# One pool of four 2 KB rooms in place of a pool of three and a pool of one, in a transformer block with an attention and an NF4 feed-forward half

## The chip, the cores and the metric

The kernel runs on one core of one Trainium2 chip. The metric is the device time of one execution in microseconds (us). Of the kernel before there are three timed runs: 3039.47, 3035.39 and 3045.34 us, median 3039.47. One further execution was profiled; all rows below are from it.

## What is computed

One block over a sequence of S = 2048 rows of E = 1024 values, in float32. First half: layer norm, attention with 16 heads of 64 values (rotary positions on queries and keys, causal mask), output projection, layer norm, and the residual. Second half: layer norm, a gated feed-forward layer with I = 2752 whose weights are stored as 4-bit codes with a scale for each 64 of them, layer norm, residual.

```
q, k, v = x @ Wq, x @ Wk, x @ Wv          # 16 heads of 64
q, k    = x*cos + rotate_every_two(x)*sin
out     = softmax(causal(q @ k.T) / 8) @ v   -> @ Wo
W       = NF4[codes] * scales             # gate, up, down
y       = (silu(h @ Wg.T) * (h @ Wu.T)) @ Wd.T
x = x + layernorm(attention(layernorm(x)));  x = x + layernorm(ffn(layernorm(x)))
```

## The kernel before, in words

Every float32 product is done as two or three matmuls on a high and a low part: `split` (L117) makes the parts, the high one by a ScalarE copy and the low one by a VectorE subtraction; `mm3` (L110) issues the three matmuls.

**Rooms.** On-chip memory is divided by hand into tags (`SLOTS`, L70); each tag has a number of rooms of one size. `slot` (L74) asks for a room. Two tags have rooms of 2 KB a partition:

- `t2`, three rooms: `t1` and `sh`, the work of the rotary embedding in `qkv` (L229 to L246); the five lookup lines `ln` of each `looked_up` (L512 to L518); the scales of the first gate and up weights (L550); `u` of the last, half-filled tile (L582).
- `ol`, one room: `ol`, the sum of the two halves of a head's weighted values (L316 to L319), written by ScalarE, added to by VectorE and stored by a DMA; the codes of the first gate and up weights (L550); `s3`, a difference of two gated tiles, made by GpSimd and stored by a DMA (L597 to L599).

The banks of PSUM are tags too (L71): `F` has one bank, for the products of `qkv` and for their transposes; `O` has one, for the weighted values; `S` and `T` have three each.

**What sets the order.** The program is traced in the order of the text. When it is built, a scheduler plays it against a timeline and fixes a static order for each engine: an instruction goes as soon as its engine, its inputs and its rooms are there, the earlier one in the text first. The rooms of one tag are given out in the order in which the text first writes the tiles: a tile doesn't get a room before each earlier tile of its tag has had one, even while rooms stand empty. On the chip, each engine runs its own instructions in that static order.

**Attention.** Eight pairs of heads. For each head and each 512-column block J of queries, `attend` (L365) runs `scores` (L252: products, mask, maxima on VectorE, exponentials on ScalarE, normalisation on GpSimd) and then `weighted` (L303): transposes of the probabilities, `split` into `pw`, products into bank `O`, then `ol`. A pair has eight `ol` tiles.

Between these lie the q, k and v products of later pairs. A *group* is the three products of one pair m and one 512-row block c (`group`, L374; `qkv`, L219). Each product fills bank `F`, is copied to `t1`, and goes on through rotary work to a store; `load_x` fetches its input into the four `xc` rooms. In the pairs 0 to 5 the groups stand in the text after all eight attends of their pair (L407 to L413), and `pace` (L409) spreads their first matmuls over that pair's scores:

```
for i, (m, c) in enumerate(now):
    ...
    group(m, c, None if i or own else ready, pace)
```

So the text of a pair has eight `ol` tiles first, and then five `t1` and `sh` tiles for each of three groups (four in pair 0). Pairs 6 and 7 have single groups between their attends (L396, L437), pair 6 two more at its end. Pair m can start only when the groups of m have stored their keys: the groups (4,3), (5,3) and (6,0) are those of the pairs 3, 4 and 5.

**Output projection**, then x2, the transposed input of the second half (L424 to L561).

**Gate and up.** 22 tiles n. For each, `gate_up` (L565) runs for four blocks c: two products of 24 matmuls each, Silu, product, store. For n even it also makes `s3` after c = 1 and c = 3. The loop that sets the order of the text is

```
for n in range(NIT):
    if n < NIT - 2:
        for c in range(NC):
            gate_up(*todo[n], c)
    if n + 1 < NIT:
        now, steps = gate_up_weights(n + 1)
        todo.append(now)
        for step in steps:
            step()
    for j in range(2):
        down_weights(n // 2, 2 * (n % 2) + j)
```

Each step of `gate_up_weights` is one `looked_up` with five `ln` tiles and a `split`; a tile n has four of them, and two more in `down_weights`. **Down** (L739) are seven products of a Strassen-like scheme on the stored tiles; it uses neither tag.

Of the kernel before, what the change touches and what calls it, by code (L numbers as in the profile page):

```python
# [10 lines left out]
F32 = mybir.dt.float32  # L11
# [11 lines left out]
D = 64  # L23
I = 2752
P = 128
# [27 lines left out]
def it_cols(it):  # L53
    return 256 if it < NIT - 1 else 128
# [3 lines left out]
def block_kernel(ctx, tc, x, wq, wk, wv, wo, gu_codes, gu_scales, d_codes, d_scales, cos_sin, out):  # L58
# [8 lines left out]
    ps = ctx.enter_context(tc.tile_pool(name="ps", bufs=1, space=PSUM))  # L67


    SLOTS = {"hd": (7, 8), "w": (3, 8), "xc": (4, 8), "pa": (6, 8), "pb": (2, 4), "f4": (4, 4), "pw": (3, 4), "t2": (3, 2), "ol": (1, 2)}  # L70
    BANKS = {"F": 1, "S": 3, "T": 3, "O": 1}  # L71
    BANK_ORDER = ("F", "S", "S", "S", "T", "T", "T", "O")

    def slot(tag, shape, dtype, name):  # L74
        assert int(np.prod(shape[1:])) * 4 <= SLOTS[tag][1] * 1024, (tag, shape)
        return sb.tile(shape, dtype, tag=tag, name=name, bufs=SLOTS[tag][0])

    def bank(tag, name="bk"):
        return ps.tile([P, 512], F32, tag=tag, name=name, bufs=BANKS[tag])
# [3 lines left out]
    def any_bank():  # L83
        turn[0] += 1
        return bank(BANK_ORDER[turn[0] % 8])
# [24 lines left out]
    def mm3(o, w, xx, first, last):  # L110

        r = T.matmul(o, lhsT=w[:, 0], rhs=xx[:, 0], start=first, stop=False)  # L112
        T.matmul(o, lhsT=w[:, 0], rhs=xx[:, 1], start=False, stop=False)  # L113
        T.matmul(o, lhsT=w[:, 1], rhs=xx[:, 0], start=False, stop=last)  # L114
        return r

    def split(hi, lo, src):  # L117
        A.copy(hi, src)  # L118
        return V.tensor_tensor(lo, src, f32(hi), ALU.subtract)  # L119
# [183 lines left out]
    def weighted(h, J, prob, v):  # L303
        o = bank("O", "o")
        nk = 4 * J + 4
        for kb in range(nk):
            j0 = max(0, kb - 4 * J)
            pt = bank("T", "pt")
            for j in range(j0, 4):
                T.transpose(pt[:, j * P : (j + 1) * P], prob[kb // 4][:, j, kb % 4 * P : (kb % 4 + 1) * P], ident)  # L310
            cs = slice(j0 * P, 512)
            pw = slot("pw", [P, 2, 512], FR, "pw")
            split(pw[:, 0, cs], pw[:, 1, cs], pt[:, cs])
            T.matmul(o[:, cs], lhsT=v[:, kb, :], rhs=pw[:, 0, cs], start=kb == 0, stop=False)  # L314
            T.matmul(o[:, cs], lhsT=v[:, kb, :], rhs=pw[:, 1, cs], start=False, stop=kb == nk - 1)  # L315
        ol = slot("ol", [D, 512], F32, "ol")  # L316
        A.copy(ol, o[D:P, :])
        V.tensor_tensor(ol, o[:D, :], ol, ALU.add)
        load(at[J][h * D : (h + 1) * D, :], ol)  # L319
# [45 lines left out]
    def attend(h, J, q, k, v, anchors):  # L365
        weighted(h, J, scores(J, q, k, anchors), v)
# [12 lines left out]
    for pair in range(KE - 1):  # L379
        anchors = []  # L380
        now = [later[g] for g in range(len(later)) if g * (KE - 1) // len(later) == pair]
# [115 lines left out]
    def looked_up(codes, s0, s1, rows, tags=None, m=None):  # L497

        if tags:
            c8, sc = (slot(tag, [P, 512], F32, "cs") for tag in tags)  # L500
        else:
            cs = slot("pw", [P, 2, 512], F32, "cs")
            c8, sc = cs[:, 0], cs[:, 1]
        for r in range(0, P, rows):
            load(c8[r : r + rows].bitcast(I32), codes)
        load(sc[:D], s0.partition_broadcast(D))
        load(sc[D:], s1.partition_broadcast(D))
        if m is None:
            m = slot("f4", [P, 2, 512], F32, "m")[:, 0]
        V.tensor_scalar(c8, c8.bitcast(I32), 1.0, -8.0, ALU.mult, ALU.add)  # L510

        def line(ab):  # L512
            ln = slot("t2", [P, 512], F32, "ln")
            if ab[2] == 1.0:
                A.activation(ln, c8, AF.Identity, bias=bias_of[ab], scale=ab[0])
            else:
                A.activation(ln, c8, AF.Prelu, bias=bias_of[ab], scale=ab[0], alpha=ab[2])  # L517
            return ln  # L518

        low = line(CODES_6_8)  # L520
        V.scalar_tensor_tensor(m, line(CODES_9_12), CODES_9_12[3], low, ALU.add, ALU.max)
        V.scalar_tensor_tensor(m, line(CODES_2_5), CODES_2_5[3], m, ALU.add, ALU.min)
        V.tensor_tensor(m, m, line(CODES_0_1), ALU.min)
        V.scalar_tensor_tensor(m, line(CODES_13_15), CODES_13_15[3], m, ALU.add, ALU.max)  # L524
        V.tensor_tensor(m, m, sc, ALU.mult)
        return m

    def gate_up_weights(n, tags=None):
        it = PAIRS[n]
        w = it_cols(it)  # L530
        wt = [slot(tag, [P, 2, 4, w], FR, "wt") for tag in ("hd", "pa" if n % 2 else "hd")]
        kk = 512 // w

        def columns_of(k0):
            n = kk * w
            off = it * KE * 256 + k0 * w
            t = wt[k0 // 4][:, :, k0 % 4 : k0 % 4 + kk, :]
            m = looked_up(
                gu_codes[:, off : off + n], gu_scales[0:1, off : off + n], gu_scales[1:2, off : off + n], P, tags
            )  # L540
            split(t[:, 0].rearrange("p k n -> p (k n)"), t[:, 1].rearrange("p k n -> p (k n)"), m)

        return (it, wt, w), [partial(columns_of, k0) for k0 in range(0, KE, kk)]
# [3 lines left out]
    new_x2(0, ["hd"] * 4)  # L547
    new_x2(1, ["pa"] * 4)
    fills = list(range(8))
    now, steps = gate_up_weights(0, ("ol", "t2"))  # L550
    todo = [now]
    for t in range(NEWX, NT):
        project_out(t, False)
# [11 lines left out]
    def gate_up(it, wt, w, c):  # L565
        g = any_bank()

        def product(o, a):
            for k in range(KE):
                mm3(o, wt[k // 4][:, :, k % 4, a : a + P], x2[c][k], k == 0, k == KE - 1)  # L570

        product(g, 0)
        kt, later, grp, odd = it % half, it // half, c // 2, c % 2
        if (kt, later, grp) not in rooms:
            rooms[kt, later, grp] = slot("f4" if later else "pb", [P, 2, 512], F32, "in")
        inter = rooms[kt, later, grp][:, odd]
        rows = P if w == 256 else D
        if w == 256:
            u = any_bank()
            product(u, P)  # L580
        else:
            u = slot("t2", [P, 512], F32, "u")[:D]  # L582
            A.copy(u, g[D:P])
            G.memset(inter[D:], 0.0)
        A.activation(inter[:rows], g[:rows], AF.Silu)  # L585
        V.tensor_tensor(inter[:rows], u, inter[:rows], ALU.mult)
        have.add((kt, grp, later, odd))

        def keep(name, tile_):
            load(aq[name][kt][:, grp], tile_)  # L590

        if (later, odd) != (0, 1):
            keep(("A11", "A12", "A22")[later + odd], inter)

        first = rooms[kt, 0, grp]
        if later == 0 and {(kt, grp, 0, 1 - odd)} <= have:
            s3 = slot("ol", [P, 512], F32, "s3")  # L597
            G.tensor_tensor(s3, first[:, 0], first[:, 1], ALU.subtract)
            keep("S3", s3)  # L599
        if {(kt, grp, a, b) for a in range(2) for b in range(2)} <= have:  # L600
            second = rooms[kt, 1, grp]
            G.tensor_tensor(first[:, 1], first[:, 1], second[:, 1], ALU.add)
            keep("S1", first[:, 1])
            G.tensor_tensor(first[:, 0], first[:, 1], first[:, 0], ALU.subtract)
            keep("S2", first[:, 0])
            G.tensor_tensor(second[:, 0], second[:, 0], first[:, 0], ALU.subtract)
            keep("S4", second[:, 0])
# [35 lines left out]
# [11 lines that stand above are left out]
# [20 lines left out]
    for c in (1, 0, 2, 3):  # L674
        for it in todo[NIT - 2 :]:
            gate_up(*it, c)
        if c == 0:

            for kt in range(2):
                ready["A11", kt] = fetch("A11", "B11", kt, True)  # L680
# [123 lines left out]
```

## Time and profile before

| What | Value |
|---|---|
| Median of the three runs | 3039.47 us |
| The profiled execution | 3038.32 us |
| Its span, first to last instruction | 3036.5 us |
| Granted TensorE clock, mean | 0.988 |
| Busy: PE, VectorE (DVE), ScalarE (ACT), GpSimd (POOL) | 96%, 67%, 56%, 31% |
| Start of the first attend's `ol`, end of the last | 188.5, 1511.6 us |
| `s3`, first and last | 1680.2, 2599.4 us |
| PE busy in 1680 to 2500 us (gate and up) | 820.0 of 820.0 us |

The span is 1.8 us shorter than the execution's own time. In the rows, PE is TensorE's matmuls, PEld its weight loads; Lnnn is the line of the kernel; "SPq" is the queue from which nearly all DMAs are issued. In a list of what waited, "x <- y: us, times" is the idle time of x's engine that y ended.

### The profile page before, as it was taken

The numbers are of one execution on the slowest core, as the hardware profiler recorded it, in microseconds if no ns is written. First come the engines' busy times: TensorE is split into PE (matmuls) and PEld (weight loads), VectorE is DVE, ScalarE is ACT, GpSimd is POOL, SyncE is SP. The second block draws the span as 40 slices with busy tenths as digits, with TensorE's granted clock in tenths as the row PEclk, the third lists the DMA queues.
The fourth block names the chain that finished last, engine by engine and source line by source line (L and its number), as shares of the span: only waits on it lengthen the run. The fifth ranks groups of instructions, "written<-read, shape, count | busy, mean of one in ns | idle before, by whom it ended". The sixth has DMA issues, their size and how long they took to land.

```text
span 3036.5 us, 42534 instructions
## 1 busy us (share of the span) xinstructions
PE 2918.4 (96%) x14168; PEld 2409.9 (79%) x14168; DVE 2033.8 (67%) x4171; ACT 1699.7 (56%) x3569; POOL 955.5 (31%) x1055
## 2 busy tenths in 40 slices
PE   7989999999999999989989999999999999899998
PEld 6868888787877787778767888888888888788887
DVE  6567778777867777777565666776666668344347
ACT  4256667676766666676555555665555556232234
POOL 5344344443444443453322122222221213100034
PEclk9999999999999999999999999999999999999999
DMA  8787666656557557472356344444433445644446
GB/s 292 270 264 233 205 212 196 192 191 205 155 193 200 191 169 229 137 241 81 104 191 215 122 139 135 152 137 134 143 122 130 137 138 180 215 136 152 146 146 232
DMA packets 271740, 536.01 MB, mean 177 GB/s; under 512 B 22944, under 2 KB 113056, under 8 KB 255648
## 3 DMA queue, kind: packets, MB, share of 16 engines
q1 hardware_dynamic: 269344, 529.10, 54.1%
q10 hardware_dynamic: 2176, 4.19, 0.4%
q8 instruction: 112, 1.84, 0.3%
q14 instruction: 108, 0.88, 0.1%
HBM read 371.98 MB, written 161.22 MB: 176 GB/s over the span
## 4 chain that ended last, share of the span: by engine, by line
PE 78%; DMA 9%; DVE 6%; ACT 3%; issue 2%; POOL 1%; SPq 0%; POOLq 0%; ACTq 0%; DVEq 0%
PE bk L112 13%; PE bk L114 13%; PE bk L113 13%; PE pt L310 6%; PE qkv L112 5%; PE qkv L113 5%; PE qkv L114 5%; PE o L315 4%; PE o L314 3%; PE s L268 3%; PE s L270 3%; DMA wf<-in_wq 2%; DMA xc<-xd 1%; PE pj L458 1%; PE pj L456 1%
## 5 line engine op out<-in xcount | busy, mean ns | idle before, releaser
L300 POOL TENSOR_SCALAR prob<-prob,rc 128x512 f32<-128x512 f32 (+3 forms) x640 | 406.0, 657 | 434.1 <-DVE rc L295 231.1
L113 PE MATMUL bk<-x,wt 128*128 128x512 f32 x1376 | 535.6, 389 | 0.0
L114 PE MATMUL bk<-x,wt 128*128 128x512 f32 x1376 | 535.2, 389 | 0.0
L112 PE MATMUL bk<-x,wt 128*128 128x512 f32 x1376 | 533.6, 389 | 1.1 <-ACT wt L118 0.9
L278 ACT ACTIVATE prob<-s,mxs 128x512 f32<-128x512 f32 (+3 forms) x640 | 402.5, 632 | 146.1 <-DVE mxs L276 91.5
L119 DVE TENSOR_TENSOR pw<-pt,pw 128x512 fp32r<-128x512 f32 (+3 forms) x640 | 378.3, 601 | 121.8 <-ACT pw L118 120.1
L118 ACT CAST pw<-pt 128x512 fp32r<-128x512 f32 (+3 forms) x640 | 324.1, 527 | 171.6 <-PE pt L310 141.0
L517 ACT ACTIVATE ln<-cs,bias 128x512 f32<-128x512 f32 x520 | 359.6, 716 | 108.0 <-DVE m L524 23.4
L310 PE MATMUL pt<-ident,prob 128*128 128x128 f32 x2176 | 346.1, 275 | 6.2 <-DVE pw L119 4.9
L310 PEld LDWEIGHTS pt<-ident,prob 128*128 128x128 f32 x2176 | 267.9, 142 | 61.2 <-issue 6.6
L112 PEld LDWEIGHTS bk<-x,wt 128*128 128x128 f32 x1376 | 258.2, 188 | 55.4 <-ACT wt L118 1.9
L114 PEld LDWEIGHTS bk<-x,wt 128*128 128x128 f32 x1376 | 258.3, 188 | 53.8
L113 PEld LDWEIGHTS bk<-x,wt 128*128 128x128 f32 x1376 | 258.2, 188 | 53.5
L276 DVE TENSOR_REDUCE mxs<-s 128x1 f32<-128x512 f32 x384 | 260.8, 681 | 59.4 <-PE s L270 58.0
L268 PE MATMUL s<-k,q 128*128 128x512 f32 (+3 forms) x640 | 265.0, 415 | 22.8 <-ACT prob L278 20.1
L315 PE MATMUL o<-pw,v 128*128 128x512 f32 (+3 forms) x640 | 247.3, 388 | 11.2 <-DVE pw L119 10.6
L314 PE MATMUL o<-pw,v 128*128 128x512 f32 (+3 forms) x640 | 244.2, 382 | 9.2 <-ACT pw L118 7.2
L112 PE MATMUL bk<-bt,at 128*128 128x512 f32 x616 | 239.9, 391 | 9.9 <-ACT in L585 8.2
L112 PE MATMUL qkv<-xc,w 128*128 128x512 f32 x576 | 230.9, 401 | 11.9 <-ACT w L179 6.8
L113 PE MATMUL bk<-bt,at 128*128 128x512 f32 x616 | 240.6, 391 | 0.0
L114 PE MATMUL bk<-bt,at 128*128 128x512 f32 x616 | 239.7, 391 | 0.0
L270 PE MATMUL s<-k,q 128*128 128x512 f32 (+3 forms) x640 | 235.6, 370 | 0.0
(146 smaller groups left out, 5512.8 us busy)
## 6 DMA issues: line engine op xcount, KB each, us to landing
xc<-xd SPq DMA_DIRECT2D x96, 1024.0 KB, 9.1
q<-qs SPq DMA_DIRECT2D x128, 256.0 KB, 7.0
ast<-S SPq DMA_DIRECT2D x44, 512.0 KB, 3.9
cs<-in_gu_scales SPq DMA_DIRECT2D x172, 128.0 KB, 3.2
cs<-in_gu_codes SPq DMA_DIRECT2D x86, 256.0 KB, 3.0
A<-in SPq DMA_DIRECT2D x66, 256.0 KB, 2.0
S<-in SPq DMA_DIRECT2D x66, 256.0 KB, 3.2
ast<-A SPq DMA_DIRECT2D x33, 512.0 KB, 4.5
```

What stands on the lines that cost most here:

```text
L112: r = T.matmul(o, lhsT=w[:, 0], rhs=xx[:, 0], start=first, stop=False)
L113: T.matmul(o, lhsT=w[:, 0], rhs=xx[:, 1], start=False, stop=False)
L114: T.matmul(o, lhsT=w[:, 1], rhs=xx[:, 0], start=False, stop=last)
L119: return V.tensor_tensor(lo, src, f32(hi), ALU.subtract)
L268: mm = T.matmul(s, lhsT=q[:, 0, j * P : (j + 1) * P], rhs=k[:, b:e], start=True, stop=False)
L270: T.matmul(s, lhsT=q[:, 1, j * P : (j + 1) * P], rhs=k[:, b:e], start=False, stop=True)
L278: A.activation(prob[i][:, j, : e - b], s, AF.Exp, bias=mx, scale=sign, accum_out=sums[:, j % BATCH, i : i + 1])
L300: G.tensor_scalar(p, p, rc[:, jj % BATCH, i : i + 1], 0.0, ALU.mult, ALU.add)
L310: T.transpose(pt[:, j * P : (j + 1) * P], prob[kb // 4][:, j, kb % 4 * P : (kb % 4 + 1) * P], ident)
L314: T.matmul(o[:, cs], lhsT=v[:, kb, :], rhs=pw[:, 0, cs], start=kb == 0, stop=False)
L315: T.matmul(o[:, cs], lhsT=v[:, kb, :], rhs=pw[:, 1, cs], start=False, stop=kb == nk - 1)
L517: A.activation(ln, c8, AF.Prelu, bias=bias_of[ab], scale=ab[0], alpha=ab[2])
```

## The change

`ol` is dropped as a tag. Its one room goes to `t2`, which has four, and its three users ask for `t2`. Nothing else is changed: the same instructions on the same engines, the same memory.

```
-    SLOTS = {"hd": (7, 8), "w": (3, 8), "xc": (4, 8), "pa": (6, 8), "pb": (2, 4), "f4": (4, 4), "pw": (3, 4), "t2": (3, 2), "ol": (1, 2)}
+    SLOTS = {"hd": (7, 8), "w": (3, 8), "xc": (4, 8), "pa": (6, 8), "pb": (2, 4), "f4": (4, 4), "pw": (3, 4), "t2": (4, 2)}
...
-        ol = slot("ol", [D, 512], F32, "ol")
+        ol = slot("t2", [D, 512], F32, "ol")
...
-    now, steps = gate_up_weights(0, ("ol", "t2"))
+    now, steps = gate_up_weights(0, ("t2", "t2"))
...
-            s3 = slot("ol", [P, 512], F32, "s3")
+            s3 = slot("t2", [P, 512], F32, "s3")
```

## The prediction

> **What bounds the kernel now.** I read the page, then the chain that ended last, then what waits around `ol`, then windows of the stages. The page gives PE as the bound: busy for 96% of the span, 78% of the chain.
>
> ```profile
> PE 2918.4 (96%) x14168; PEld 2409.9 (79%) x14168; DVE 2033.8 (67%) x4171; ACT 1699.7 (56%) x3569; POOL 955.5 (31%) x1055
> ...
> PE 78%; DMA 9%; DVE 6%; ACT 3%; issue 2%; POOL 1%; SPq 0%; POOLq 0%; ACTq 0%; DVEq 0%
> ```
>
> So all idle time of PE is 3036.5 - 2918.4 = 118 us. What the one `ol` room costs is in the list of what waited around that tile:
>
> ```profile
> L317 ACT COPY ol<-o x64: 582/584/589, 188.5 to 1511.6; 64x512 f32<-64x512 f32 x64
> ...
>   DMA at<-ol: 11.8, 5
> ...
> DMA to landing us min/median/max: 2.2/6.2/12.4
> ```
>
> Five of 64 copies wait for the last store, 11.8 us of ScalarE. PE's gaps just behind these and two shorter waits (0.59, 2.00, 2.24, 0.99, 0.74, 0.58, 0.53 us) are 7.7 us. That is all there is to win there.
>
> Next, three stretches that a pair of heads each takes (columns: start and end, length, then busy PE, PEld, DVE, ACT, POOL with counts, granted clock, DMA share, GB/s):
>
> ```profile
> 541.00:695.00 154.00, 151.50 (x831) 127.82 (x831) 118.34 (x304) 104.37 (x278) 67.93 (x92) 0.98 0.63 192
> 695.00:855.00 160.00, 153.24 (x821) 125.86 (x822) 121.57 (x316) 109.14 (x290) 66.27 (x93) 0.98 0.62 188
> 855.00:1021.00 166.00, 154.61 (x825) 125.78 (x826) 121.36 (x317) 109.43 (x293) 66.70 (x94) 0.99 0.61 184
> ```
>
> Of the mean 153 us of PE, the nine q, k, v products (24 matmuls each, 0.23 us from start to start) are 50 us and their transposes 1.5; attention is about 101. These 50 us are what PE does while it waits for VectorE and ScalarE.
>
> **The rule that decides.** Rooms of a tag go out in the order of the text. The queue shows it, around the first lookups:
>
> ```profile
> 1335.50 1.04 SPq L507 DMA_DIRECT2D cs<-in_gu_scales  x1
> ...
> 1512.97 0.45 SPq L319 DMA_DIRECT2D at<-ol  x1
> 1515.24 0.34 SPq L505 DMA_DIRECT2D cs<-in_gu_codes  x1
> ...
> 1524.45 0.49 SPq L506 DMA_DIRECT2D cs<-in_gu_scales  x1
> ```
>
> The scales of step 1 take a `t2` room at 1335, when the last `t1` has had its own. Those of step 2 need nothing, and two of three rooms stand empty for 180 us, yet they come only at 1524, when the lines of step 1 (the first at 1518.4) have had their rooms. So in the pool of four every `t1`, `sh` and `ln` queues behind each earlier `ol` and `s3`, whatever is free. The number of rooms hardly matters; the order does.
>
> **Part 1, `s3` among the lookup lines.** In the text, `s3` of the last block of an even tile n stands before the lines of n+1. Now they run the other way round (n = 2):
>
> ```profile
> 1752.85 1.32 ACT L517 ACTIVATE ln<-cs,bias 128x512 f32<-128x512 f32 x2
> ...
> 1784.03 0.71 ACT L517 ACTIVATE ln<-cs,bias 128x512 f32<-128x512 f32 x1
> ```
> ```profile
> 1794.13 1.29 POOL L598 TENSOR_TENSOR s<-in 128x512 f32<-128x512 f32 x1 [2.83 <-issue]
> ```
>
> All six steps (30 lines in 31 us, 5.1 us a step) end 10 us before that `s3`. With one pool they come behind it, that is, behind the last product of tile n, while PE wants the weights of n+1 at once. PE's wait for the first step: the product L586 0.68, five VectorE operations L521 to L525 at 0.68, ScalarE's copy L118 0.60, some seven hand-overs of 0.1: 5.4 us, and up to 1 us for lines in between: 6.5. Below: 5.4, if ScalarE has all lines ready. Above: 9, if no line starts before `s3` itself. The later steps come at 5.1 us each, while one step's weights give PE 8 products x 6 matmuls x 0.23 = 11 us in eight banks: no further wait. PE has nothing else to do in this stage; VectorE and ScalarE, 69% and 56% busy in 1680 to 2500, have room for the shifted work, and what stands behind the lines on ScalarE (Silu of later blocks) isn't held up, since the order is made so that the lines are placed later rather than waited for. The loads of codes and scales are in other rooms (`pw`) and stay early on the queue; the store of `s3` stays where it is. It happens for n = 0, 2 to 18: ten times; for odd n there is no `s3`.
>
> After such a gap the matmuls are slow. The nearest row:
>
> ```profile
> 2601.07 0.39 PE L113 MATMUL bk<-bt,at 128*128 128x512 f32 x1
> 2609.68 0.80 PE L112 MATMUL bk<-bt,at 128*128 128x512 f32 x1 [8.22 <-ACT in L585]
> ...
> 2614.54 0.63 PE L113 MATMUL bk<-bt,at 128*128 128x512 f32 x1
> ...
> 2615.26 0.39 PE L112 MATMUL bk<-bt,at 128*128 128x512 f32 x1
> ```
>
> 5.6 us at a granted clock of 0.50: 13 matmuls in the time of 24, a loss of 2.6 us. The Trainium skill ("TensorE: Matmul & The Clock Gate", section "What's actually happening") has full clock again after some 3.4 us of work, a loss of 1.7. By the rule ten stalls would cost 17 us more, by the row 26; I take the row. Sum: 10 x (6.5 + 2.6) = 91 us (54 + 17 = 71 to 90 + 26 + ten slips of 2 = 136).
>
> **Part 2, `ol` among the rotary rooms.** A pair's eight `ol` stand before its groups' `t1`. So the first product of a pair fills the one bank `F` and waits there for the last attend; the other eight come in a bunch behind it. Now the products of such a pair are spread evenly (the `t1` copies of pair 2 start at 559.1, 572.0, 582.8, 602.5 and so on to 682.6).
> - Attention alone: stretches without one q, k, v matmul exist already:
>
> ```profile
> 464.90:486.80 21.90, 21.23 (x130) 17.54 (x128) 20.67 (x56) 19.73 (x54) 8.41 (x15) 1.00 0.70 270
> 621.20:643.20 22.00, 21.06 (x132) 17.69 (x131) 19.79 (x57) 19.35 (x53) 8.72 (x15) 1.00 0.68 264
> 780.10:803.30 23.20, 22.46 (x138) 18.52 (x137) 21.42 (x58) 20.48 (x56) 7.85 (x14) 1.00 0.74 251
> ```
>
>   PE holds 96.5%, VectorE 92%: 3.6 us idle in 101, within today's 7 a pair. Little is lost here.
> - Groups in a bunch: with one bank, PE waits for copy and hand-over (0.8 us), at the third product for copy, transposes and `split` too (2.7): 4.3 a group. The input of the next group (four tiles, 9.1 us to landing) can only follow the last product, on the one queue that the three stores of the bunch, their 0.5 MB tables and the next keys share: some 4 more. Nineteen groups of pairs 0 to 5 x 8.3 = 158. The next pair's scores fill part: one `O` bank and six `prob` rooms let it run a short attend, 16 and 8 units of scores, 17 us, behind pairs 0 and 1; 10 behind pair 2, 5 behind 3 and 5, 0 behind 4, whose own groups are what pair 5 waits for: 54. Left 104. The two at the end of pair 6: 16 - 5 = 11.
> - Latency laid bare: from a k product to scores it is rotary work 5.3 (0.6 + 0.74 + 0.68 + 2 x 1.3 and `split`), store 9.2, load 7.1: 22 us, of which one v product covers 6.4. Before pair 5: 15.5 + 3 to start up. Before J = 3 of pair 6 and J = 2 of pair 7, where attend and group strictly alternate: 22 each. Before J = 3 of pair 7 the projection fills: 5. Sum 68.
> - Slow clock, 2.6 for about 12 of these gaps: 31.
> - Given back: of PE's 43 us idle in 190 to 1345, about 30 are counted anew above, the 7.7 of the `ol` waits among them.
>
> Sum 104 + 11 + 68 + 31 - 30 = 184 us (80 if the next pair fills nearly all; 310 if it fills nothing and the inputs' 4 MB a group queue up).
>
> The first lookups (codes and scales both in `t2`): each step still follows the last; 0, between -3 and +5.
>
> A rule of the Trainium skill speaks for the change: "Perfetto Trace Analysis", section "Optimization Strategy", has bubbles that repeat as a sign of too few buffers. By it the win is the 7.7 us of gaps, and half of 13.6 us at a clock of 0.50 behind two of them (539.8 and 696.8): -15. The same section advises to interleave regimes; the rows above price the loss of that. I follow the rows.
>
> **Sum.** 3036.5 + 91 + 184 = 3311.5 of span, + 1.8 around it = 3313 for an execution like the profiled one, + 1.2 to the median: 3314 us, 9% slower.
>
> **Rivals.**
> - *Only the lookups suffer* (3130 to 3220, at 3170): the bunched groups of a pair find cover in the next pair's attention. 91 + 40. For: a pair's attention needs the groups of its own m only, two pairs ahead at first. Against: the single bank `O`.
> - *Strict alternation* (3410 to 3520, at 3470): 310 and 126. Against: two pairs of scores do run ahead.
> - *The waits go and nothing else changes* (3025, faster): 15 us less, at the copies of `ol` at 343 to 1261. It decides if a rotary copy may take a room that an earlier `ol` hasn't asked for yet. The scales at 1524 speak against it.
> - *No effect* (3039): a change of rooms that the order absorbs.
>
> **Chances.** The forecast (3220 to 3410) 0.62; only lookups 0.17; alternation 0.12; faster 0.04; within 0.3%, about what a measurement of this kernel can tell from no change, 0.03; slower by less than 3% 0.02. The range leaves out these last 0.09, the lower part of the second and the top of the third: 3140 to 3450.
>
> **What would show it.** After: no `ln` line between the start of an even tile and its second `s3`; ten PE gaps of 5 to 9 us between 1900 and 2900, ended by L118 or L119, each with half clock behind; all `t1` copies (L231, L241) of pairs 0 to 5 in bunches behind the eighth L317; waits for `at<-ol` gone. Wrong, if `t1` copies stay spread between the `ol` copies, or if PE's gaps in gate and up are under 3 us.

## The result and the profile after

The kernel after takes 3471.64 us (median of four runs, 3471.47 to 3475.19), the kernel before 3039.86 beside it: a ratio of 1.1422, 95% interval 1.1402 to 1.1442. The change costs 432 us. Forecast were 3314, range 3140 to 3450: the sign holds, the size lies above the range. The profiled execution has a span of 3469.6 us at a mean granted clock of 0.951. The page of the kernel after, its busy times and the shares of the chain that ended last:

```profile
PE 3063.3 (88%) x14168; PEld 2453.8 (71%) x14168; DVE 2064.3 (59%) x4171; ACT 1696.3 (49%) x3569; POOL 957.6 (28%) x1055
...
PE 65%; DMA 12%; DVE 7%; ACT 5%; issue 4%; POOL 4%; SPq 2%; POOLq 0%; ACTq 0%; DVEq 0%
```

The counts are those of before, and so are the busy times of ScalarE and GpSimd. TensorE is idle for 406 us (before: 118), and its records cover 145 us more for the same 14168 matmuls. Around the tile `ol`:

```profile
L317 ACT COPY ol<-o x64: 582/583/587, 195.7 to 1861.9; 64x512 f32<-64x512 f32 x64
...
  ACT ol L317: 15.7, 14
...
DMA to landing us min/median/max: 2.2/2.2/14.0
```

The waits for the store (`at<-ol`) are gone, and its median landing fell from 6.2 to 2.2 us. But the last `ol` starts at 1861.9 where it was 1511.6.

**Where the time went.** From the first `ol` to the last, the attention, 1666.2 us against 1323.1: +343. From the last `ol` to the end 1607.7 against 1524.9: +83. Gate and up, from the first `s3` to the last, has +91 of that (1009.9 against 919.2); behind it 7 come back. The first `ol` itself starts 7 us later. It does so in every run with four rooms in `t2` (195.2 to 199.5 us) and in none with three (187.4 to 189.5); why stays open.

*Gate and up.* TensorE's rows around one gap (start, duration, then what is computed; in brackets the idle time and what ended it):

```profile
2145.82 0.39 PE L114 MATMUL bk<-x,wt 128*128 128x512 f32 x1
2153.35 0.80 PE L112 MATMUL bk<-x,wt 128*128 128x512 f32 x1 [7.14 <-ACT wt L118]
2153.94 0.63 PE L113 MATMUL bk<-x,wt 128*128 128x512 f32 x1
```

Ten such gaps of 7.13 to 7.15 us stand behind the even tiles 0 to 18, each ended by the high part of the next weights. GpSimd's row shows the second `s3` of that tile, ScalarE's the lookup lines:

```profile
2147.09 1.64 POOL L598 TENSOR_TENSOR s<-in 128x512 f32<-128x512 f32 x1 [20.47 <-DVE in L586]
```
```profile
2141.30 1.94 ACT L517 ACTIVATE ln<-cs,bias 128x512 f32<-128x512 f32 x3
2147.64 0.72 ACT L515 ACTIVATE ln<-cs,bias 128x512 f32<-128x512 f32 x1 [4.40 <-DVE m L521]
...
2152.69 0.60 ACT L118 CAST wt<-m 128x512 fp32r<-128x512 f32 x1
```

Before, all thirty lines of the next tile ended 10 us ahead of the `s3`. Now three start 6 us ahead of it, right behind the last Silu, and the others behind it. From one even tile to the next the first `s3` comes 96.4 us later (the mean from tile 2, at 2125.3, to tile 18, at 2896.6), before 87.0: 9.4 us a time. The gap is 7.1 of it. Behind a gap TensorE works at half clock for 2.8 to 6.1 us, 4.1 in the mean, which loses half of that, 2.0. Two of these stretches (same columns as below; PE was busy all through):

```profile
2153.35:2156.60 3.25, 3.25 (x8) 2.57 (x9) 3.25 (x6) 3.25 (x6) 0.00 (x0) 0.50 0.31 115
2345.10:2351.16 6.06, 6.06 (x14) 4.79 (x15) 5.96 (x10) 6.00 (x10) 0.00 (x0) 0.50 0.38 128
```

*Attention.* The bunch of groups ahead of pair 2, the eight attends of pair 2, then the bunch ahead of pair 5 (length, busy PE, PEld, DVE, ACT, POOL with counts, granted clock, DMA share, GB/s):

```profile
515.40:585.80 70.40, 58.44 (x258) 44.92 (x258) 30.33 (x73) 21.22 (x53) 31.82 (x34) 0.98 0.69 236
585.80:680.40 94.60, 88.29 (x512) 71.01 (x512) 77.86 (x198) 72.42 (x191) 31.84 (x52) 1.00 0.17 58
1079.00:1196.90 117.90, 70.25 (x277) 52.70 (x277) 29.41 (x66) 24.85 (x58) 20.30 (x16) 0.83 0.79 237
```

The work has come apart. In the second window run the attends and a single product, the one that fills bank `F` and waits there: DMA 17% busy, VectorE 82%. In the first and third nearly all is products (attention has 11 of the 58 us of PE's work, and 10 of the 70): DMA 69% and 79%, VectorE 43% and 25%, and TensorE waits. The `t1` copies stand in bunches at 516.0 to 585.2, 681 to 778.7 and so on, between the eighth `ol` of a pair and the first of the next. What ended TensorE's idle time in the attention (total us, times, longest):

```profile
PE qkv L112 <- DMA xc<-xd: 48.4, 23, 4.7
PE s L268 <- DMA q<-qs: 46.3, 8, 29.8
PE qkv L112 <- ACT w L179: 38.6, 3, 13.6
PE s L268 <- ACT prob L278: 34.7, 60, 1.8
PE qkv L112 <- ACT t L241: 31.0, 39, 1.3
```

Before, the first four are 4.4, 1.1, 6.8 and 18.7, and the fifth doesn't occur. The inputs of the next group, the queries, the weights of the next pair, the single bank: before, each was in time or nearly so.

### The profile page after: what moved, and what is told of

Same layout as the page of the kernel before. It is cut to its first block, busy times and chain, and to the rows that moved or that the text cites. A ratio compares the mean times of both kernels' runs of the same rounds, so it can differ in the third digit from the quotient of the medians.

```text
span 3469.6 us, 42668 instructions
## 1 busy us (share of the span) xinstructions
PE 3063.3 (88%) x14168; PEld 2453.8 (71%) x14168; DVE 2064.3 (59%) x4171; ACT 1696.3 (49%) x3569; POOL 957.6 (28%) x1055
## 4 chain that ended last, share of the span: by engine, by line
PE 65%; DMA 12%; DVE 7%; ACT 5%; issue 4%; POOL 4%; SPq 2%; POOLq 0%; ACTq 0%; DVEq 0%
PE bk L112 12%; PE bk L113 12%; PE bk L114 12%; PE pt L310 5%; DMA xc<-xd 4%; PE qkv L112 3%; PE o L315 3%; PE s L268 3%; PE o L314 3%; PE qkv L114 3%; PE qkv L113 3%; PE s L270 2%; ACT prob L278 2%; DVE mxs L276 1%; DMA q<-qs 1%
## 5 line engine op out<-in xcount | busy, mean ns | idle before, releaser
L300 POOL TENSOR_SCALAR prob<-prob,rc 128x512 f32<-128x512 f32 (+3 forms) x640 | 397.5, 648 | 614.8 <-DVE rc L295 245.5
L517 ACT ACTIVATE ln<-cs,bias 128x512 f32<-128x512 f32 x520 | 348.4, 715 | 69.4 <-DVE mb L521 33.3
L268 PE MATMUL s<-k,q 128*128 128x512 f32 (+3 forms) x640 | 276.7, 434 | 106.9 <-DMA q<-qs 46.3
L112 PE MATMUL qkv<-xc,w 128*128 128x512 f32 x576 | 250.7, 435 | 136.0 <-DMA xc<-xd 48.4
L112 PEld LDWEIGHTS bk<-x,wt 128*128 128x128 f32 x1376 | 266.2, 194 | 132.9 <-ACT wt L118 77.2
L113 PEld LDWEIGHTS bk<-x,wt 128*128 128x128 f32 x1376 | 265.4, 193 | 55.8
L114 PEld LDWEIGHTS bk<-x,wt 128*128 128x128 f32 x1376 | 258.5, 188 | 54.5 <-DVE wt L119 0.9
L315 PE MATMUL o<-pw,v 128*128 128x512 f32 (+3 forms) x640 | 251.1, 394 | 12.3 <-DVE pw L119 11.6
L314 PE MATMUL o<-pw,v 128*128 128x512 f32 (+3 forms) x640 | 252.9, 395 | 9.1 <-ACT pw L118 7.0
L112 PEld LDWEIGHTS qkv<-xc,w 128*128 128x128 f32 x576 | 117.0, 203 | 189.5 <-DMA xc<-xd 58.6
L268 PEld LDWEIGHTS s<-k,q 128*128 128x128 f32 x640 | 126.4, 197 | 174.3 <-ACT prob L278 106.0
L270 PE MATMUL s<-k,q 128*128 128x512 f32 (+3 forms) x640 | 242.4, 380 | 0.0
L114 PE MATMUL qkv<-xc,w 128*128 128x512 f32 x576 | 241.2, 419 | 0.0
```

What stands on the lines that cost most here:

```text
L268: mm = T.matmul(s, lhsT=q[:, 0, j * P : (j + 1) * P], rhs=k[:, b:e], start=True, stop=False)
L300: G.tensor_scalar(p, p, rc[:, jj % BATCH, i : i + 1], 0.0, ALU.mult, ALU.add)
```

## The experiments

The theory: the order of the text on one tag's rooms, not their number, is the cause; `s3` holds back the lookup lines, and `ol` holds back the `t1`. The main rival in size was strict alternation of attends and groups. "Before" is near 3040 us in each comparison; times in brackets are 95% intervals of the ratio.

**1. `ol` alone** (the kernel before, three rooms in `t2`):

```
-        ol = slot("ol", [D, 512], F32, "ol")
+        ol = slot("t2", [D, 512], F32, "ol")
```


> Only the weighted values ol move into the pool, which stays at three rooms; s3 and the first codes keep the single room. Theory of order (rooms go out in the order of the text): all of what the change costs in attention and nothing of what it costs in gate and up: 3039.9 + 432 - 88 = 3384 us (3365 to 3405), no gap of PE over 3 us between tiles in gate and up. Rival, crowding (rooms are short, the order is harmless): with a room fewer than the changed kernel, attention at least as slow, and gate and up slowed too through lines that wait for rooms: over 3420.

Measured 3405.13 us, ratio 1.1193 (1.1172 to 1.1214): +365, at the upper edge of what order forecast. No gap in gate and up. The attention is 1669.2 us long, as after.

**2. `s3` alone** (before, three rooms):

```
-            s3 = slot("ol", [P, 512], F32, "s3")
+            s3 = slot("t2", [P, 512], F32, "s3")
```


> Only s3 moves into the pool, which stays at three rooms; ol and the first codes keep the single room. Order: ten gaps of 7.1 us and 1.7 us of slow clock behind each, nothing else: 3039.9 + 88 = 3128 us (3118 to 3138). Crowding: s3 holds a room for some 4 us twice in 87 us, so 3040 to 3050. Rival, a link between the halves (attention's order moves gate and up): under 3100.

3137.42 us, 1.0314 (1.0298 to 1.0330): +98, with ten gaps of 7.75 us. With the fourth room they are 7.13: the pool's fourth room is worth 0.6 us a gap. The work at half clock behind them is 3.5 and 5.8 us by turns, a loss of 2.3 in the mean.

**3. `s3` asked for later in the text** (after; the second `s3` of an even tile stands behind the next lookups and `down_weights`):

```
-                gate_up(*todo[n], c)
+                gate_up(*todo[n], c, defer=c == 3)
...
+        while late:
+            make_s3(*late.pop())
```


> The pool of four as in the change, but the second s3 of each even tile stands behind the lookups of the next tile in the text instead of ahead of them; nothing else. Order: the ten gaps of PE in gate and up go, attention stays: 3471.6 - 88 = 3384 us (3375 to 3400). Crowding, or a wait for GpSimd: the gaps stay, 3455 to 3475.

3380.07 us, 1.1113 (1.1096 to 1.1130): 92 us under the kernel after, with all four rooms still in one pool, and no gaps. So in gate and up the place in the text is the whole cause.

**4. The gaps of 2 filled** with useless matmuls ahead of the first product of each odd tile (nine fall into the gaps), to price the clock:

```
+        if it >= half and c == 0 and w == 256:
+            for _ in range(28):
+                T.matmul(g, lhsT=x2[c][0][:, 0, :P], rhs=x2[c][1][:, 0], start=True, stop=True)
```


> The kernel with only s3 in the pool (3137 us), with 28 useless matmuls of 128x512 ahead of the first product of each odd tile, into the bank that this product then overwrites: 28 x 0.22 = 6 us of the 7.75 us gap. Theory that 2 us behind each gap are the slow clock: nine gaps filled, the clock stays at 1.00 there, 3137 - 9 x 2.0 = 3119 (3112 to 3128) although TensorE does more. Rival, the 2 us are the later steps of the lookups, not the clock: 3137 or more.

3123.57 us, 1.0275 (1.0260 to 1.0290): 13.9 us under 2, although TensorE does 280 matmuls more. The same stretch in 2 and then here (same columns as above):

```profile
1720.00:2690.00 970.00, 899.03 (x3864) 738.69 (x3863) 614.11 (x893) 490.23 (x774) 194.72 (x132) 0.96 0.39 129
```
```profile
1720.00:2690.00 970.00, 955.77 (x4201) 787.20 (x4199) 626.85 (x913) 501.32 (x792) 199.69 (x133) 1.00 0.41 134
```

The granted clock goes from 0.96 to 1.00, and more VectorE and ScalarE work fits into the same 970 us. The 13.9 us are not the price of nine gaps: the tenth filling ran at 1666.0, where there was no gap, and the attention, which the edit doesn't touch, is 6 us longer in this profile than in that of 2. The price is read within the stage. From one second `s3` of an even tile to the next, over eight filled gaps, it takes 95.2 us, in 2 97.3: half clock behind a gap of 7.8 us costs 2.1.

**5. `ol` in the pool for the pairs 0 to 5 alone** (before):

```
-        ol = slot("ol", [D, 512], F32, "ol")
+        ol = slot("t2" if h < 12 else "ol", [D, 512], F32, "ol")
```


> ol moves into the pool of three for heads 0 to 11 only; heads 12 to 15, s3 and the first codes keep the single room. Theory that the strict alternation of attends and groups in pairs 6 and 7 is what the forecast missed: the part of pairs 0 to 5 is what was forecast for it, 120 to 170, so 3160 to 3210, at 3190. Rival, a like price for each pair: 6/8 of 344, so 3298 (3270 to 3320).

3293.42 us, 1.0826 (1.0805 to 1.0848): +254, and so 112 of the 365 belong to the pairs 6 and 7. My theory had put much more on these two pairs; the rival, a like price for every pair, was right.

**6 and 7. Every second head's `ol` in the pool** (before, three rooms). With the even heads a pair's groups may start once its first head is through, and have the second head beside them; with the odd heads they wait for the pair's end. The edit is that of 6; 7 has `if h % 2` in its place.

```
-        ol = slot("ol", [D, 512], F32, "ol")
+        ol = slot("t2" if h % 2 == 0 else "ol", [D, 512], F32, "ol")
```


> Pool of three; only the ol of the first head of each pair moves into it, the second head's stay in the single room with s3. Theory of lost cover (the groups cost time because nothing runs beside them): the groups wait for the fourth ol only and then run beside the second head's attends, so most of the cost of ol in the pool (365 us with all of them) goes: 3040 + 60 = 3100 us (3070 to 3150). Rival, the bunch itself (one bank F, the inputs' loads, the queue) is what costs, whatever runs beside it: 3250 or more.

> Pool of three; only the ol of the second head of each pair moves into it. The groups wait for the eighth ol as in the change, but the next pair's first head isn't held by them. Lost cover: covered where the next pair doesn't need these groups (behind pairs 0 and 1, half of 2), bare elsewhere: 3040 + 200 = 3240 us (3180 to 3300). Rival, it is the ol held back behind the groups that costs, not the t1 held back behind the ol: near 3100. Rival, the bunch itself: 3380 or more.

Even heads 3167.82 us, 1.0415 (1.0399 to 1.0432): +126. Odd heads 3329.37, 1.0949 (1.0929 to 1.0969): +288. Both lie above their range, by 18 and 29 us; but the even heads are the cheaper, and both stay under the rival of the bunch itself (3250 and 3380), as lost cover has it. With the even heads the pairs 1 to 4 have 5.7 to 9.5 us of TensorE's idle time each, before 1.8 to 11.9: a bunch with attends beside it adds next to no idle time (TensorE's records in the attention still cover 40 us more). What is left is one gap of 30 us ahead of pair 5 and 68 us of idle time in the pairs 6 and 7. With the odd heads the pairs 3, 4, 5 and 7 have 32, 40, 55 and 65 us.

**8. The text put into the order of time** (after, pool of four; the products of the groups stand one by one between the attends, all 24 groups in the pairs 0 to 6, at a lower priority; `s3` as in 3):

```
+                while made < count and made * PACE * 8 < done * count:
+                    later_on(next, between)
+                    made += 1
...
-        if J in (1, 2):
-            group(m, J + 1)
```


> The pool of four as in the change, with the text put into the order of time: the products of the groups stand one by one between the attends of their pair (all 24 groups in the pairs 0 to 6), at low priority, and the second s3 of an even tile behind the next tile's lookups. Theory of order: it is back at the kernel before, less up to 15 us for the waits of ol that are gone: 3035 us (3015 to 3080). Crowding or a fault of the shared pool itself: over 3250.

3044.82 us (20 runs) against 3041.33 (23 runs), 1.0015 (1.0007 to 1.0023). All but 3.5 of the 432 us are gone with the single pool kept. The waits for `at<-ol` are gone too, and yet nothing is won. Why isn't shown: the text differs from that of before as well, and the same text with two tags was not run.

**9. One room fewer** (after, three rooms; the first codes and scales go to a room of `pw`):

```
-"t2": (4, 2)}
+"t2": (3, 2)}
...
-    now, steps = gate_up_weights(0, ("t2", "t2"))
+    now, steps = gate_up_weights(0)
```


> The changed kernel with three rooms in the one pool instead of four (the first codes and scales in a room of pw). Theory of order: as slow as the change, plus what the two parts had more with three rooms each (365 + 98 - 432 = 31): 3502 us (3475 to 3520); the gaps in gate and up 7.7 us, not 7.1. Rival, crowding: a quarter of the rooms less makes it far worse, over 3560.

3528.30 us, 1.1606 (1.1581 to 1.1631): +57, 8 above the range. 14 of it are in the attention, 53 behind it (the output projection waits 28.5 us for ScalarE's split of its input, the gaps are 7.8 us), less 8 ahead of the first `ol`. `pw` is also where the projection's results lie, so how much of the wait for the split is the room and how much the move of the codes isn't separated. The number of rooms is worth 57 us at most here, their order hundreds.

**10. `ol` in the pool of `pw`** (before), which the same attend also uses, to see whether a shared pool is free when text and time agree:

```
-        ol = slot("ol", [D, 512], F32, "ol")
+        ol = slot("pw", [D, 512], F32, "ol")
```


> The kernel before with ol in a room of pw instead of its own: in the text and in time, ol stands behind its own head's pw tiles, so the order of the pool is the order of time. Theory of order: a shared pool costs nothing, the five waits for the store of ol go, a room of three is held some 7 us per attend: 3025 to 3055, at 3037. Rival, sharing itself costs: over 3090.

A miss: 3132.23 us, 1.0308 (1.0291 to 1.0325), +94. Who waited for the tile `ol` (us, times), and what ended ScalarE's wait (us, times, longest):

```profile
  ACT pw L118: 101.4, 37
```
```profile
ACT pw L118 <- DMA at<-ol: 101.4, 37, 6.3
```

The copies into `pw` wait until the store of an `ol` has landed: `ol` keeps one of the three rooms for that long (5.7 us in the median from the store's issue). So users in order can still hold each other up, through a room that a store keeps. The next attend's first `pw` also stands behind this attend's `ol` in the text, while two attends overlap in time; how much of the 94 us is that order and how much the room held isn't separated.

**11 to 14. Waits of a bunch taken away one by one**, to split the 344. In 11 the weights of pair 2 serve all groups (the loads and splits of 15 weights are left out). In 12 all 24 groups stand in the bunches behind the pairs 0 to 6. In 13 both; in 14, besides, the first group's inputs serve all groups (the other loads of inputs are left out too). The edit at `group` is that of 11 and 13, with `inputs[0]` for the inputs in 14; the one at `later` goes with the single groups of pair 7 in 12 to 14.

```
-        if m not in ws:
-            ws[m] = prep_qkv(m)
-        qkv(m, c, ws[m], xs or load_x(c), pace=pace)
+        if not ws:
+            ws[2] = prep_qkv(2)
+        qkv(m, c, ws[2], xs or load_x(c), pace=pace)
...
-    later = [(m, c) for m in range(2, KE) for c in range(NC)][:-2]
+    later = [(m, c) for m in range(2, KE) for c in range(NC)]
```


> The changed kernel, with the weights of pair 2 prepared once and used for the groups of pairs 3 to 7 too (it leaves out fifteen loads of weights and their splits). Theory that the forecast missed the weights' place in the bunch (three gaps of 12 to 14 us behind them, and their loads ahead of keys and queries in the queue): 45 to 75 us less than the change, 3472 - 60 = 3412. Rival, weights are hidden behind other waits that then show: 3450 to 3472.

> The changed kernel with all 24 groups in the bunches behind the pairs 0 to 6, none between the attends of the pairs 6 and 7, and with that no pair whose groups are all wanted at once by the next. Theory that the forecast's latency term was too small (data of a group wanted by the very next attend: before pair 5, in the pairs 6 and 7): 3472 - 130 = 3342 us (3310 to 3370). Rival, the bunches cost alike wherever they stand: 3440 or more.

> The kernel after with all 24 groups in the bunches behind the pairs 0 to 6 (as in e11) and, besides, every group of the pairs 2 to 7 using the weights of pair 2 (as in e6). It leaves out 15 loads and splits of weights, so its output is not the block's. e11 alone took 52 us off, e6 alone 25. Theory that the waits of a bunch cover one another (take one away and the next one in the same bunch ends the gap): the two together give about what each gives alone, 52 + 25, so 3395 (3385 to 3410). Rival, that they add up: the waits for ScalarE's copies of the weights were 53 us in e11, and with the half clock behind them (four gaps over 13 us, 1.6 each) 59 us go: 3360 (3350 to 3370).

> e12 with the inputs of its first group kept for all groups, so that no xc tile is loaded after it; it leaves out 20 loads of inputs, besides the weights. What is left in a bunch is the single bank F with its copy, transposes and split, and what the next pair's attention waits for. Theory that the inputs are the largest wait of a bunch (48 us of TensorE's idle time in the kernel after ended with them, 55 with the weights once): 45 to 60 us under e12, with the waits for bank F at 4.3 us a group left over. Rival, that bank F, the copies and the hand-overs set the pace of a bunch and the inputs only come last by a little: under 25 us below e12.

| Run | us | ratio, 95% | attention, us | idle in it |
|---|---|---|---|---|
| after | 3471.64 | 1.1402 to 1.1442 | 1666.2 | 286.9 |
| 11 weights once | 3446.28 | 1.1300 to 1.1353 | 1635.5 | 259.6 |
| 12 groups ahead | 3419.84 | 1.1216 to 1.1271 | 1616.4 | 243.4 |
| 13 both | 3380.25 | 1.1089 to 1.1146 | 1573.3 | 204.1 |
| 14 inputs once as well | 3292.81 | 1.0811 to 1.0859 | 1483.0 | 146.6 |

What ended TensorE's idle time in the attention, in 12, in 13 and in 14:

```profile
PE qkv L112 <- ACT w L179: 53.0, 4, 13.6
PE qkv L112 <- DMA xc<-xd: 49.4, 19, 5.2
```
```profile
PE qkv L112 <- DMA xc<-xd: 63.5, 27, 5.5
PE s L268 <- ACT prob L278: 31.8, 49, 5.2
PE qkv L112 <- ACT t L241: 29.3, 39, 1.3
```
```profile
PE s L268 <- ACT prob L278: 28.1, 54, 2.1
PE qkv L112 <- ACT t L241: 25.4, 34, 1.3
PE qkv L112 <- DVE vo L119: 20.7, 11, 1.9
```

None of the four came out as expected: 25 us instead of 60 in 11, 52 instead of 130 in 12, in 13 40 under 12, between the two theories' 25 and 60, and in 14 87 under 13 instead of at most 60. A wait taken away is handed on in part: without the weights (53 us) the inputs rise from 49 to 64. The inputs, taken away third, are the largest step of the row. Behind them the bank stays: copy, transposes and split, 56 us in 14 with the transposes' own wait of 10.3.

## Why the prediction was right in kind and wrong in size

**The mechanism: right.** Rooms go out in the order of the text: experiments 3 and 8 undo the cost with the pool unchanged (3 its part in gate and up, 8 all but 3.5 us), 1 and 2 bring it back with three rooms. The three rivals of little or no cost fall: *only the lookups suffer*, *the waits go and nothing else changes*, *no effect*.

**Part 1, `s3` among the lookup lines: right.** Forecast 10 x (6.5 + 2.6) = 91 us; measured 92 by experiment 3, and 91 from the first `s3` to the last. The parts were off against each other: the wait is 7.1, not 6.5, and the slow clock 2.0 in the mean, not 2.6. The estimate of 1.7, from the 3.4 us of work at half clock in the Trainium skill ("TensorE: Matmul & The Clock Gate", "What's actually happening"), lies 0.3 below the mean, where the row lies 0.6 above it: TensorE works 2.8 to 6.1 us at half clock here. The row that I took was one of the long ones. Its window granted at half clock was 10.2 us long; behind the ten gaps two are of that length and eight 6.8, and each begins 2.5 to 4.2 us before TensorE resumes (6.8 us from 2149.8, say, with TensorE back at 2153.35). Of the signs named, one failed: three lookup lines still come ahead of the second `s3`.

**Part 2, `ol` among the rotary rooms: the step that failed.** "Sum 104 + 11 + 68 + 31 - 30 = 184 us"; measured 344 in the change (432 less 88), 343 of it between the first and the last `ol`. It took TensorE's idle time and a dozen slow stretches as the whole loss, and left out what a bunch has to load and prepare itself. Short by 159 us: 60 of idle time, 18 of the give-back, 30 of slow clock and 51 that had no term. By its terms:

| Term | forecast | measured | where from |
|---|---|---|---|
| idle in the bunches of pairs 0 to 5, the gap ahead of pair 5 with them | 104 + 18.5 | 149 | windows between the eighth `ol` and the next pair's first |
| idle in pairs 6 and 7 | 11 + 22 + 22 + 5 | 94 | window 1376.1 to 1861.9 |
| given back of today's idle | -30 | -12 | 43.7 left elsewhere, 55.5 before |
| slow clock | 31 | 61 | busy at half clock 147.7 less 25.4, halved |
| TensorE's records longer at full clock | not listed | 51 | busy +112, less the 61 |
| Sum | 184 | 343 | |

- *The bunches* were priced about right: 26 us too low. The fill by the next pair's attention took place: 57 us of TensorE's work ahead of the bunches' last products, forecast 54. That the sum fits is luck in part, since by pairs it is 11, 11, 22, 1, 4 and 8 where 17, 17, 10, 5, 0 and 5 stood. *"Attention alone: little is lost"* holds: 5.7 to 9.9 us idle in each window of eight attends, pairs 0 to 5.
- *Not listed: the weights in the bunch.* The weights of the next pair load and are split in the bunch now (gaps of 13.0, 13.6 and 11.9 us); before, an attend ran beside that. Taken away they are worth 25 us alone, 40 in company. The third of these gaps lies in pair 6.
- *"Latency laid bare"*, 18.5 us ahead of pair 5, is a gap of 29.8. From the end of the k product to the first scores it takes 37.6 us, not 22. The queue at that time (start, duration on SP, DMA):

```profile
1149.64 5.40 SPq L172 DMA_DIRECT2D wf<-in_wk  x1
1155.09 4.74 SPq L239 DMA_DIRECT2D vs<-vo  x1
...
1165.14 12.36 SPq L332 DMA_DIRECT2D q<-qs  x8
```

  I had counted rotary work and the landing times of one store and one load. On the one queue the loads of keys and queries stand behind weights and the store of v, and these three rows alone take SP 22.5 us.
- *The slow clock* counted 12 gaps by 2.6 us. In the bunches it comes behind many short waits, not a dozen long ones: half clock holds in 34 stretches of the attention and for 147.7 us of TensorE's work, before in 5 and for 25.4.
- *Matmuls that come singly.* A matmul's record is 0.39 us, the next starts after 0.23 when it stands ready. TensorE's records in the attention are broken 312 times after, 104 before: 208 x 0.16 = 33 us of record tails, an estimate that explains so much of the 51. I had read idle time alone as the loss. The rest of the 51 stays open.
- *Given back*: the idle time of before sits in the attends (ScalarE's exponentials, VectorE's `pw`), and these run as before.

Taken away in a row, what was late in a bunch splits the other way: late groups 50 us of the attention's length, weights 43, inputs 90, and 160 that remain in 14 for the single bank, the chains of copies and the clock. These are differences in one order of removal; in another they'd come out otherwise, as 11 against 13 shows (25 and 40 for the same step). How the 344 split exactly stays open.

**The rival that came nearest.** *Strict alternation* gave 3470, and the time is 3471.6. It isn't shown right by that: it assumed that the next pair fills nothing, and 11 us of attention do run in each of the bunches behind the pairs 0 and 1, and 22 in that behind pair 2. (Its 126 for part 1 isn't the 136 that the forecast's own range ends with; with that it would have been 3485.) Its larger price stood in for the terms that I hadn't listed. At 0.12, with a range that ended in its middle, it had too little weight.

**The other rule.** The Trainium skill's "Perfetto Trace Analysis" ("Optimization Strategy") takes bubbles that repeat as a sign of too few buffers. The bubbles at `at<-ol` did go in the pool of four, and nothing was won by it: in experiment 8 they are gone too, and the ratio is 1.0007 to 1.0023. That they'd be worth nothing with all else the same isn't shown.

## What to carry to other kernels

Where rooms of a tag are given out in the order of the text, two users should share a tag only if their order in the text is also their order in time (and even then one can hold up the other, through a room that a store keeps: experiment 10); look for the pairs of instructions that run the other way round in the trace, and ask what the later one hides. To price work that loses its cover, add to its waits what has to be loaded and prepared inside it, the queue's own time, and TensorE's busy time, which grows too when matmuls come singly or at half clock: here 112 of 343 us were no idle time. Before merging rooms, count what the wait is worth: here 11.8 us of ScalarE's waiting went, and not even with the text put in order was anything won.

## What the runs showed of the hardware

- Behind a gap of 7.1 us TensorE worked 2.8 to 6.1 us at half clock (a loss of 2.0 in the mean), behind one of 7.8 us 3.5 or 5.8 (2.3), not for the whole window granted at half clock (6.8 or 10.2 us), of which 2.5 to 4.5 us lay in the gap itself. 28 useless matmuls in the gap won 2.1 us each time (97.3 to 95.2 us from one even tile to the next, experiments 2 and 4).
- SP took 5.40 us over one weight load whose neighbour took 0.39, and 12.36 over eight query loads: the hand-over from the k product to the first scores took 37.6 us, where rotary work and the landing times of one store and one load had made 22.
